# Layer 0's attention in halves: Gram blocks of 16 columns, softmax by banks, first tiles mixed ahead

## The chip, the cores and the metric

The kernel runs on one core of a Trainium2 chip. The metric is the time of one execution on the device, in microseconds (us), as the median of several runs; a profile comes from one execution of its own. TensorE (PE; its weight loads are shown as PEld) multiplies, VectorE (DVE), ScalarE (ACT) and GpSimd (POOL) do the elementwise work, and SyncE's queue (SP) issues the DMAs.

## The reference, cut to what matters

The program is two transformer layers on x of shape 4 x 512 x 1024, in fp32. Layer 0's attention, the part that the change touches, works for each of the 1024 columns on its own: the four batch rows of a column attend to each other over the 512 positions. Ahead of it the rows of x are normalised, and its result is added to x.

```python
q = jnp.transpose(x, (2, 0, 1))                       # column, n, position
scores = jnp.einsum('lnc,lmc->lnm', q, q) / c ** 0.5  # 4 x 4 for each column
prob = jax.nn.softmax(scores, axis=-1)
msg = jnp.einsum('lnm,lmc->lnc', prob, q)
return x + jnp.transpose(msg, (1, 2, 0))
```

Layer 0's FFN follows: a layer norm, a product with W_base, gate and LoRA inputs (1160 columns in all), a top-2 routing and the LoRA outputs. Then layer 1's attention with 32 heads and layer 1's FFN, which the change does not touch.

## The kernel before, in words

x lies in SBUF as 16 tiles of 128 rows by 1024 columns; tile n * 4 + j holds rows j * 128 to j * 128 + 127 of batch row n. The tiles are loaded in the order of the row blocks j (L62), so the four tiles of block 0 come first.

For each row block j the kernel takes the tiles' mean and variance (`statistics`: ACT with two passes over a tile, L111 and L113, for one or two of the four tiles, DVE with L119 and L120 for the others; then `rsqrt`, L93 to L100), and normalises the four tiles (L130) into a layout of 32 groups. A group g has 128 columns: 32 columns of x for each of the four batch rows. The first 20 groups go to `hA`, the last 12 to `hB`, of which all four row blocks are kept.

TensorE turns each group (L255), four to a PSUM tile, and ACT copies them out (L257) to `hTA` and `hTB`. It multiplies each group with itself (L259 for the 20 groups of hA, summed over the row blocks in the five PSUM banks `gA`). The 12 groups of hB are multiplied after the last row block (L267, three banks `gB`), since there is no PSUM for them before that. A Gram block is 128 x 128, of which only the entries with the same column matter: a 4 x 4 block for each column.

`weights` works on one bank of four groups: a mask times the Gram block (L195), a sum that leaves 4 x 4 scores for each column (L198), the softmax in small operations, and the weights spread out again over a 128 x 128 block with its identity added (L212, by DVE or POOL). `turned` transposes them (L219) and ACT copies them (L221). `mix` multiplies a row block of four groups by the weights (L230), and DVE adds the product to x (L233). There are 8 x 4 mixes: first all four row blocks of the 20 groups of hTA, then row block after row block of the rest.

The weights of layer 0's FFN, `w0`, come in eight chunks of 128 x 1160. Each is loaded to a stage (L168), ACT makes the rounded part (L171) and POOL the remainder (L172). The first four are loaded to memory that hA and hB leave, through two stage buffers, the last four to memory that hTA leaves, through three.

Once the first row block is mixed, the tiles of row block 0 get their statistics for the FFN (L300), and the first two tiles are normalised (L463 to L465), transposed (L152) and split (L134, L135). Then the FFN's products begin: `base` (L305) takes, for each of the three column groups of a tile, all eight chunks in order, with three products each (`matmul3`, L139 to L141). POOL adds the bias to x (L497).

A scheduler orders each engine's instructions by the program's order and its own estimates; `tc.high_priority` and `tc.issue_after` are hints to it. Engines run their queues in order.

Of the kernel before, what the change touches and what calls it, by code (L numbers as in the profile page):

```python
# [17 lines left out]
P = 128  # L18
# [15 lines left out]
GW = 32  # L34
# [11 lines left out]
def block_kernel(ctx: ExitStack, tc: tile.TileContext, a: dict, out: bass.AP):  # L46
# [31 lines left out]

    same_col = const.tile([P, GW], F32, name="same_col")
    V.tensor_copy(same_col, ident[:, 0:GW])  # L80
    for n in range(1, NB):
        V.tensor_tensor(same_col, same_col, ident[:, n * GW : (n + 1) * GW], ALU.add)
    same_n = const.tile([P, NB], F32, name="same_n")
    V.tensor_reduce(same_n, ident.rearrange("p (n l) -> p n l", n=NB), AX.X, ALU.add)
# [5 lines left out]
    def rsqrt(v, n, eps, name="y2", bufs=3):  # L90

        root = small.tile([P, n], F32, name="root")
        A.activation(root, v, AF.Sqrt, bias=epsilons[eps])  # L93
        y = small.tile([P, n], F32, name="y")
        V.reciprocal(y, root)
        t = small.tile([P, n], F32, name="nt")
        V.scalar_tensor_tensor(out=t, in0=y, scalar=-0.5, in1=y, op0=ALU.mult, op1=ALU.mult)
        V.scalar_tensor_tensor(out=t, in0=v, scalar=eps, in1=t, op0=ALU.add, op1=ALU.mult)
        y2 = small.tile([P, n], F32, name=name, bufs=bufs)
        V.scalar_tensor_tensor(out=y2, in0=t, scalar=1.5, in1=y, op0=ALU.add, op1=ALU.mult)  # L100
        return y2
# [27 lines left out]
    def normalise(dst, xt, mv, rstd, k):  # L129
        return V.tensor_scalar(dst, xt, mv[:, k, 0:1], rstd[:, k : k + 1], ALU.subtract, ALU.mult)  # L130
# [34 lines left out]
    def load_split(pool, stage, src, shape, name, eng=None):  # L165

        raw = stage.tile(shape, F32, name="stage")
        nc.sync.dma_start(out=raw, in_=src)  # L168
        hi = pool.tile(shape, FR, name=f"{name}_h")
        lo = pool.tile(shape, FR, name=f"{name}_l")  # L170
        A.copy(hi, raw)  # L171
        (eng or V).tensor_tensor(lo, raw, f32(hi), ALU.subtract)  # L172
        return hi, lo

# [3 lines left out]
    NQA, NQ = GA // 4, NGR // 4  # L178
    wpools, aside = ExitStack(), ExitStack()
    with tc.tile_pool(name="a_hTB", bufs=1) as hTBp, tc.tile_pool(name="a_WB", bufs=GB // 4) as WBp, \  # L180
# [11 lines left out]
        def weights(gram, eng):  # L192

            masked = wk.tile([P, 4 * NB, GW], F32, name="masked")
            V.tensor_tensor(masked, gram.rearrange("p g (n l) -> p (g n) l", n=NB),  # L195
                            same_col.unsqueeze(1).to_broadcast([P, 4 * NB, GW]), ALU.mult)
            sc = wk.tile([P, 4, NB], F32, name="sc")
            V.tensor_reduce(sc.rearrange("p g n -> p (g n)"), masked, AX.X, ALU.add)  # L198
            top = small.tile([P, 4, 1], F32, name="top")
            V.tensor_reduce(top, sc, AX.X, ALU.max)  # L200
            ex = wk.tile([P, 4, NB], F32, name="ex")
            V.tensor_tensor(ex, sc, top.to_broadcast([P, 4, NB]), ALU.subtract)
            exps.append(A.activation(ex, ex, AF.Exp, scale=1.0 / math.sqrt(S)))
            den = small.tile([P, 4, 1], F32, name="den")
            V.tensor_reduce(den, ex, AX.X, ALU.add)
            rden = small.tile([P, 4, 1], F32, name="rden")
            V.reciprocal(rden, den)
            pr = wk.tile([P, 4, NB], F32, name="pr")
            V.tensor_tensor(pr, ex, rden.to_broadcast([P, 4, NB]), ALU.mult)
            V.tensor_tensor(pr, pr, same_n.unsqueeze(1).to_broadcast([P, 4, NB]), ALU.add)  # L210
            wt = wk.tile([P, 4 * NB, GW], F32, name="wt", bufs=3)
            eng.tensor_tensor(  # L212
                wt, pr.rearrange("p g n -> p (g n)").unsqueeze(2).to_broadcast([P, 4 * NB, GW]),
                same_col.unsqueeze(1).to_broadcast([P, 4 * NB, GW]), ALU.mult)
            return wt.rearrange("p (g n) l -> p g (n l)", g=4)

        def turned(wt, ps, Wp):
            for g in range(4):
                T.transpose(ps[:, g, :], wt[:, g, :], ident)  # L219
            w = Wp.tile([P, 4, P], F32, name="w")  # L220
            A.copy(w, ps)  # L221
            return w

        xv = x.rearrange("p (n j) (g l) -> p j g n l", n=NB, l=GW)

        def mix(q, w, j, psp):
# [5 lines left out]
            xs = xv[:, j, 4 * q : 4 * q + 4]  # L232
            V.tensor_tensor(xs, xs, ps.rearrange("p g (n l) -> p g n l", n=NB), ALU.add)  # L233

        psA, psB = ExitStack(), ExitStack()
        with tc.tile_pool(name="a_hB", bufs=1) as hBp, tc.tile_pool(name="a_hA", bufs=2) as hAp:
            gAp = psA.enter_context(tc.tile_pool(name="a_gA", bufs=1, space=PSUM))
            hB = [hBp.tile([P, GB, P], F32, name=f"hB{j}") for j in range(TPB)]
            junk = hBp.tile([P, D], F32, name="junk")
            gA = [gAp.tile([P, 4, P], F32, name=f"gA{q}") for q in range(NQA)]  # L240
            with tc.tile_pool(name="a_pt", bufs=NQ - NQA, space=PSUM, side="right") as ptp:
                for j in range(TPB):
                    hA = hAp.tile([P, GA, P], F32, name="hA")
                    xs = [x[:, n * TPB + j, :] for n in range(NB)]
                    mv, rstd = statistics(xs, junk=[junk] * (1 + j % 2))
                    for n in range(NB):
                        for dst, c0, c1 in ((hA, 0, GA * GW), (hB[j], GA * GW, D)):
                            normalise(dst.rearrange("p g (n l) -> p n g l", n=NB)[:, n],
                                      xs[n][:, c0:c1].rearrange("p (g l) -> p g l", l=GW),
                                      mv, rstd, n)  # L250
                    for q in range(NQ):
                        pt = ptp.tile([P, 4, P], F32, name="pt")
                        for g in range(4 * q, 4 * q + 4):
                            src = hA[:, g, :] if g < GA else hB[j][:, g - GA, :]
                            T.transpose(pt[:, g % 4, :], src, ident)  # L255
                        dst = hTA[:, 4 * q : 4 * q + 4] if q < NQA else hTB[:, 4 * q - GA : 4 * q - GA + 4]
                        A.copy(dst[:, :, j * P : (j + 1) * P], pt)  # L257
                    for g in range(GA):
                        T.matmul(gA[g // 4][:, g % 4, :], lhsT=hA[:, g, :], rhs=hA[:, g, :],  # L259
                                 start=(j == 0 and g % 4 == 0), stop=(j == TPB - 1),  # L260
                                 skip_group_check=True)
            gBp = psB.enter_context(tc.tile_pool(name="a_gB", bufs=1, space=PSUM, side="right"))
            gB = [gBp.tile([P, 4, P], F32, name=f"gB{q}") for q in range(NQ - NQA)]
            for q in range(NQ - NQA):
                for g in range(4):
                    for j in range(TPB):
                        T.matmul(gB[q][:, g, :], lhsT=hB[j][:, 4 * q + g, :],  # L267
                                 rhs=hB[j][:, 4 * q + g, :], start=(j == 0 and g == 0),
                                 stop=(j == TPB - 1), skip_group_check=True)
            ws = [turned(weights(g, (G, V)[q % 2]), g, WAp) for q, g in enumerate(gA)]  # L270
# [4 lines left out]
        def load_w0(pool, chunks, bufs):  # L275
            with tc.tile_pool(name="b_st", bufs=bufs, side="right") as stage:
                for ch in chunks:
                    w0.append(load_split(pool, stage, a["w0"][ch], [P, W0_COLS[-1][1]], f"w0{ch}",
                                         G))

        load_w0(w0p, range(ND // 2), 2)
        psA.close()
        with tc.tile_pool(name="a_ps", bufs=4, space=PSUM) as psp:
            ws += [turned(weights(g, (V, G)[q % 2]), g, WBp) for q, g in enumerate(gB)]
            with tc.issue_after(exps[-1].ins):
                A.activation(first, first, AF.Sqrt)
            for q in range(NQA):
                for j in range(TPB):
                    mix(q, ws[q], j, psp)
            aside.close()  # L290
            w0q = wpools.enter_context(tc.tile_pool(name="b_wB", bufs=1, side="right"))
            jp = psB.enter_context(tc.tile_pool(name="a_junk", bufs=1))
            junk = jp.tile([P, D], F32, name="junk")
            stats0 = {}
            for j in range(TPB):
                for q in range(NQA, NQ):
                    mix(q, ws[q], j, psp)
                if j == 0:
                    with tc.high_priority():
                        stats0[0] = statistics([x[:, n * TPB, :] for n in range(NB)], junk=[junk])  # L300
                    load_w0(w0q, range(ND // 2, ND), 3)
# [3 lines left out]
    def base(hts, w, cols, pop, part):  # L305

        hh, hl = hts
        po = []
        for c0, c1 in cols[part]:
            ps = pop.tile([P, 512], F32, name="po")  # L310
            for ch in range(ND):
                wh, wl = w[ch]
                matmul3(ps[:, 0 : c1 - c0], hh[:, ch, :], hl[:, ch, :], wh[:, c0:c1],
                        wl[:, c0:c1], start=(ch == 0), stop=(ch == ND - 1))
            po.append(ps)
        return po
# [98 lines left out]
    with tc.tile_pool(name="b_h", bufs=2) as hp, tc.tile_pool(name="b_hTh", bufs=2) as hTh, \  # L415
# [45 lines left out]
        def turn0(s):  # L461
            t = order[s]
            h = hp.tile([P, D], F32, name="h")  # L463
            with tc.high_priority() if s < 2 else ExitStack():
                normed.append(normalise(h, x[:, t, :], *stats0[s // NB], s % NB))  # L465
            return transposed(h, (hTh, hTl), ptp)

        normed = []
        hts = {0: turn0(0), 1: turn0(1)}
        po = {0: base(hts[0], w0, W0_COLS, pop, slice(0, 3))}  # L470
        room1 = raw()
        fetch_w1(room1, 0)
        done, mvs0, mvs1 = normed[1], {}, {}
        for s, t in enumerate(order):
# [22 lines left out]
            G.tensor_tensor(x[:, t, :], x[:, t, :], bias0, ALU.add)  # L497
# [1100 lines left out]
```

## Time and profile before

| what | value |
|---|---|
| median of 3 runs (lowest, highest) | 1797.71 us (1795.58, 1800.64) |
| the profiled execution's own time | 1795.89 us |
| its span, first to last instruction | 1794.1 us |
| mean granted TensorE clock | 0.992 |
| TensorE busy | 1734.4 us (97%) |
| VectorE busy | 1325.2 us (74%) |
| ScalarE busy | 904.1 us (50%) |
| GpSimd busy | 884.6 us (49%) |
| first matmul | 15.53 us |
| end of the Gram products, by the chain | 62.95 us |
| first product of layer 0's FFN (L139) | 110.06 us |

All times within a profile are counted from the span's start. A line of the timeline gives the start, the duration of a group of like instructions, the engine, the line of the program, the operation, what it writes and reads, and in brackets the idle time ahead of it with what ended it. A line of the windows gives a stretch, its length and the busy time of each engine in it, with the number of instructions. An fp32 product counts as two matmul records, since TensorE takes it in two passes; a transpose counts as one.

### The profile page before, as it was taken

To read this page: it belongs to the slowest core of one execution; us is meant where nothing else is said; L and a number is where in the kernel's file an instruction comes from. 1 tells how busy PE (TensorE), PEld (TensorE's weight loads), DVE (VectorE), ACT (ScalarE), POOL (GpSimd) and SP (SyncE) were. 2 spreads that over 40 slices of the span, in tenths; PEclk is the share of its full clock that TensorE was granted. 3 is DMA by queue.
4 is the path that set the end of the run, shared out by engine and by line. 5 is a ranking of instruction groups with operands and counts; after the bars stand their busy time and mean duration, and the time that the engine had idled before them with its cause. 6 is when DMAs were issued, how large, how long until landed. Compare 5 with 4: busy or idle time off the path is not lost.

```text
span 1794.1 us, 31052 instructions
## 1 busy us (share of the span) xinstructions
PE 1734.4 (97%) x10280; PEld 1449.8 (81%) x10280; DVE 1325.2 (74%) x3556; ACT 904.1 (50%) x2321; POOL 884.6 (49%) x851
## 2 busy tenths in 40 slices
PE   6979999999899999999999999999999999989999
PEld 5979999999667877767777767777766777789998
DVE  7777887576687777777777777777678777587785
ACT  6331332165665555475555565555565555453332
POOL 0352433101456566545566545666645555565453
PEclk9989999999899999999999999999999999999999
DMA  4121554236332343362242453243344323844331
GB/s 188 70 87 62 169 173 144 75 95 186 112 121 79 121 130 105 109 201 93 98 140 92 133 174 117 92 138 106 116 166 131 125 99 115 308 170 137 130 117 61
DMA packets 131937, 228.12 MB, mean 127 GB/s; under 512 B 22272, under 2 KB 58752, under 8 KB 128448
## 3 DMA queue, kind: packets, MB, share of 16 engines
q1 hardware_dynamic: 131776, 226.13, 37.6%
q8 instruction: 82, 1.34, 0.3%
q14 instruction: 79, 0.65, 0.1%
HBM read 156.60 MB, written 71.83 MB: 127 GB/s over the span
## 4 chain that ended last, share of the span: by engine, by line
PE 84%; DVE 7%; POOL 2%; DMA 2%; ACT 2%; issue 1%; SPq 0%; POOLq 0%; DVEq 0%; ACTq 0%
PE psv L851 8%; PE pst L835 7%; PE pss L139 4%; PE pss L140 4%; PE pss L141 4%; PE poa L139 3%; PE pob L139 3%; PE po L139 3%; PE po L141 3%; PE po L140 3%; PE psq L139 3%; PE psq L141 3%; PE psq L140 3%; PE poa L141 3%; PE poa L140 3%; PE pob L141 3%
## 5 line engine op out<-in xcount | busy, mean ns | idle before, releaser
L814 ACT ACTIVATE p<-p,mn 128x512 f32<-128x512 f32 (+3 forms) x512 | 284.5, 559 | 206.7 <-DVE mn L811 205.4
L634 POOL TENSOR_TENSOR qf<-qf,ropeT 64x512 f32<-64x512 f32 x128 | 165.5, 1293 | 276.5 <-ACT qf L630 272.4
L811 DVE CUSTOM_DVE_ANT_0 p<-pss,causal 128x512 f32<-128x512 f32 (+3 forms) x512 | 231.2, 485 | 33.8 <-PE pss L141 26.1
L835 PE MATMUL pst<-ident,p 128*128 128x128 f32 x1280 | 185.8, 273 | 0.7 <-ACT pT L837 0.7
L635 POOL TENSOR_TENSOR qf<-qf,t 64x512 f32<-64x512 f32 x128 | 165.7, 1294 | 41.2 <-DVE t L633 33.2
L835 PEld LDWEIGHTS pst<-ident,p 128*128 128x128 f32 x1280 | 153.6, 141 | 25.4 <-ACT pT L837 2.5
L837 ACT COPY pT<-pst 128x512 f32<-128x512 f32 x256 | 142.0, 580 | 47.7 <-PE pst L835 46.9
L643 POOL TENSOR_TENSOR ql<-qf,qh 128x384 fp32r<-128x384 f32 x128 | 130.0, 1015 | 66.8 <-DVE qh L642 66.8
L139 PE MATMUL pss<-kT,ql 128*128 128x512 f32 (+2 forms) x384 | 144.6, 377 | 4.7 <-DVE mn L811 2.0
L886 POOL TENSOR_TENSOR cxl<-s,cxh 128x256 fp32r<-128x256 f32 x128 | 97.1, 767 | 90.1 <-ACT cxh L885 64.2
L139 PE MATMUL po<-w_h,hTl 128*128 128x384 f32 (+1 forms) x384 | 133.4, 348 | 0.8 <-DVE x L339 0.8
L140 PE MATMUL pss<-kT,qh 128*128 128x512 f32 (+2 forms) x384 | 130.9, 341 | 0.0
L141 PE MATMUL pss<-kT,qh 128*128 128x512 f32 (+2 forms) x384 | 130.5, 340 | 0.0
L141 PE MATMUL po<-w_h,hTh 128*128 128x384 f32 (+1 forms) x384 | 130.2, 339 | 0.0
L140 PE MATMUL po<-w_l,hTh 128*128 128x384 f32 (+1 forms) x384 | 129.8, 338 | 0.0
L837 DVE COPY pT<-pst 128x256 f32<-128x256 f32 x128 | 54.0, 422 | 95.9 <-PE pst L835 95.5
L630 ACT COPY qf<-psq 128x512 f32<-128x512 f32 x126 | 74.0, 587 | 70.7 <-PE psq L141 69.2
L632 DVE TENSOR_TENSOR t<-psq,ropeT 32x512 f32<-32x512 f32 x126 | 87.6, 696 | 24.6 <-ACT qf L630 20.6
L139 PEld LDWEIGHTS pss<-kT,ql 128*128 128x128 f32 x384 | 72.5, 189 | 40.0 <-POOL ql L643 11.6
L814 ACT ACTIVATION_READ_ACCUMULATOR p<-p,mn 128x1 f32 x512 | 97.4, 190 | 0.0
L633 DVE TENSOR_TENSOR t<-psq,ropeT 32x512 f32<-32x512 f32 x126 | 87.1, 691 | 1.8
L928 DVE TENSOR_TENSOR xs<-xs,pob 128x512 f32<-128x512 f32 x105 | 71.2, 678 | 19.5 <-PE pob L141 19.2
(569 smaller groups left out, 5004.0 us busy)
## 6 DMA issues: line engine op xcount, KB each, us to landing
xs<-x_d SPq DMA_DIRECT2D x128, 256.0 KB
x_d<-xs SPq DMA_DIRECT2D x128, 256.0 KB
slotC<-in_woT_dram SPq DMA_DIRECT2D x32, 512.0 KB
rb<-r_d SPq DMA_DIRECT2D x128, 128.0 KB
w_t<-raw SPq DMA_DIRECT2D x32, 288.0 KB
x<-in_x_dram SPq DMA_DIRECT2D x16, 512.0 KB
x_d<-x SPq DMA_DIRECT2D x32, 256.0 KB
slotA<-q_d SPq DMA_DIRECT2D x8, 1024.0 KB
```

The lines of the kernel that those rows point to most:

```text
L139: T.matmul(ps, lhsT=al, rhs=bh, start=start, stop=False, **kw)
L140: T.matmul(ps, lhsT=ah, rhs=bl, start=False, stop=False, **kw)
L141: T.matmul(ps, lhsT=ah, rhs=bh, start=False, stop=stop, **kw)
L634: G.tensor_tensor(f[mid], f[mid], ropeT[mid, 0, :], ALU.mult)
L635: G.tensor_tensor(f[mid], f[mid], t2[mid], ALU.add)
L643: G.tensor_tensor(l, f[:, P:S], f32(h), ALU.subtract)
L811: turn_of[0] = V.tensor_tensor_reduce(out=to, in0=ps[:, 0:n], in1=causal[:, S - n : S], scale=1.0, scalar=-NEG, op0=ALU.add, op1=ALU.min, ...
L814: A.activation(to, to, AF.Exp, bias=mn[:, i : i + 1], scale=-1.0, accum_out=rs[:, i : i + 1])
L835: T.transpose(ps[:, w : w + P], p[:, OF[i] + j * P : OF[i] + (j + 1) * P], ident)
L837: copy(pT[:, AT[js[0]] : AT[js[0]] + w], ps[:, 0:w])
L851: T.matmul(ps[n * KVR : (n + 1) * KVR, S - w : S], lhsT=k[:, j, :], rhs=pTs[u + n][:, AT[j] : AT[j] + w], start=(j == 0), stop=(j == TPB - 1))
L886: G.tensor_tensor(l, src, f32(h), ALU.subtract)
```

## The change

The groups are laid out anew: a group of 128 columns is now two halves of 64, each with 16 columns of x for the four batch rows. A Gram block is two products of 64 x 64, one on each half of the array's columns, which write to the two halves of the PSUM partitions. The 32 groups' blocks so take four PSUM banks, and all of them are summed while the row blocks come; the pool `hB` and the separate `gB` products are gone. In row blocks 0 to 2 each four transposes are followed by the eight half products of the same groups; in the last row block all half products come first, and the transposes after them.

In row block 0 the statistics are taken in two sets, three tiles and one; ACT normalises part of the tiles, and the tiles are normalised in two column halves. Later blocks' statistics are to be issued after the normalisation or the root ahead of them.

The softmax works on a bank of eight groups in place of four. The spreading by columns is made in two steps (`halves`, `wt`). As soon as a set of four groups has its weights, row block 0 of the set before is mixed; then come row blocks 1 to 3 of the groups in hTA, with the statistics of the four tiles of row block 0 between them, then the two first tiles' normalisation, then the rest of the mixes. `w0`'s first chunks are to be issued after the last `wt`. For the first tile `base` takes the first four chunks for all three column groups, then the last four. POOL's bias additions are to be issued after the last split on POOL.

```diff
-    same_col = const.tile([P, GW], F32, name="same_col")
...
+    same_col = const.tile([P, GL], F32, name="same_col")
+    V.tensor_reduce(same_col, ident.rearrange("p (k l) -> p l k", l=GL), AX.X, ALU.add)
+    same_half = const.tile([P, 2], F32, name="same_half")
+    V.tensor_reduce(same_half, ident.rearrange("p (b k) -> p b k", b=2), AX.X, ALU.add)
...
+            halves = wk.tile([P, GBK, 2, NB], F32, name="halves")
+            V.tensor_tensor(halves, pr.unsqueeze(2).to_broadcast([P, GBK, 2, NB]),
+                            same_half.unsqueeze(1).unsqueeze(3).to_broadcast([P, GBK, 2, NB]),
+                            ALU.mult)
...
+            grams = [gp.tile([P, GBK, 2 * GW], F32, name=f"g{k}") for k in range(NGR // GBK)]
+            with tc.tile_pool(name="a_pt", bufs=4, space=PSUM, side="right") as ptp:
                 for j in range(TPB):
-                    hA = hAp.tile([P, GA, P], F32, name="hA")
+                    h = hp.tile([P, NGR, P], F32, name="h")
                     xs = [x[:, n * TPB + j, :] for n in range(NB)]
-                    mv, rstd = statistics(xs, junk=[junk] * (1 + j % 2))
...
+                    sets = (xs[:3], xs[3:]) if j == 0 else (xs,)
+                    norms = []
+                    with tc.issue_after((normed if j == 1 else rooted[0]).ins) if j else ExitStack():
+                        for k, part in enumerate(sets):
+                            mv, rstd = statistics(part, "", 3, [junk] * (k == 0) * (1 + (j > 1)))
...
+                            if j == 0 and n < (2 if c else 3):
+                                normed = A.activation(to, xt, AF.Identity, bias=off[:, i : i + 1],
+                                                      scale=rstd[:, i : i + 1])
+                            else:
+                                normalise(to, xt, mv, rstd, i)
...
+                    def gram(q):
+                        for g in range(4 * q, 4 * q + 4):
+                            for b in range(2):
+                                half = slice(b * 2 * GW, (b + 1) * 2 * GW)
+                                T.matmul(grams[g // GBK][half, g % GBK, :], lhsT=h[:, g, half],
+                                         rhs=h[:, g, half], start=(j == 0 and g % GBK == 0),
+                                         stop=(j == TPB - 1), skip_group_check=True)
...
+                    for q in range(NQ):
+                        if j < TPB - 1:
+                            turn(q)
+                        gram(q)
+                    if j == TPB - 1:
+                        for q in range(NQ):
+                            turn(q)
-                    for g in range(GA):
-                        T.matmul(gA[g // 4][:, g % 4, :], lhsT=hA[:, g, :], rhs=hA[:, g, :],
...
-            for q in range(NQ - NQA):
-                for g in range(4):
-                    for j in range(TPB):
-                        T.matmul(gB[q][:, g, :], lhsT=hB[j][:, 4 * q + g, :],
...
+            for k, gram in enumerate(grams):
+                halves = weights(gram)
+                for i in range(2):
+                    q = 2 * k + i
+                    w, last_wt = turned(halves, i, psp, WAp if q < NQA else WBp, (V, G)[i])
+                    ws.append(w)
+                    if q > 0:
+                        mix(q - 1, ws[q - 1], 0, psp)
+            mix(NQ - 1, ws[NQ - 1], 0, psp)
...
+            with tc.issue_after(last_wt.ins):
+                load_w0(w0p, range(ND // 2), 2, (G, G))
+            mv = small.tile([P, NB, 2], F32, name="mv", bufs=3)
+            for k, (q, j) in enumerate((q, j) for q in range(NQA) for j in range(1, TPB)):
+                mix(q, ws[q], j, psp)
+                if k % 2 and k // 2 < NB:
+                    statistic(mv, x[:, k // 2 * TPB, :], k // 2)
+            stats0 = {0: (mv, rsqrt(mv[:, :, 1], NB, 1e-5, "rstd", 3))}
             aside.close()
...
+            load_w0(w0q, range(ND // 2, ND), 3, (G, G))
+            early = []
+            for n in range(2):
+                early.append(hp.tile([P, D], F32, name="h"))
+                done = normalise(early[n], x[:, n * TPB, :], *stats0[0], n)
+            for j in range(1, TPB):
                 for q in range(NQA, NQ):
                     mix(q, ws[q], j, psp)
...
-                    with tc.high_priority():
-                        stats0[0] = statistics([x[:, n * TPB, :] for n in range(NB)], junk=[junk])
-                    load_w0(w0q, range(ND // 2, ND), 3)
...
+        for chunks in (range(ND),) if not in_halves else (range(ND // 2), range(ND // 2, ND)):
+            for ps, (c0, c1) in zip(po, cols[part]):
+                for ch in chunks:
...
-        po = {0: base(hts[0], w0, W0_COLS, pop, slice(0, 3))}
+        po = {0: base(hts[0], w0, W0_COLS, pop, slice(0, 3), True)}
...
+            with tc.issue_after(behind_split[0].ins):
+                G.tensor_tensor(x[:, t, :], x[:, t, :], bias0, ALU.add)
```

## The prediction, made before the changed kernel ran

> **What bounds the kernel now.** I read the page's chain first, then the stages of layer 0's attention by windows, then TensorE's timeline and the chain in them. The chain is 84% TensorE:
>
> ```profile
> PE 84%; DVE 7%; POOL 2%; DMA 2%; ACT 2%; issue 1%; SPq 0%; POOLq 0%; DVEq 0%; ACTq 0%
> ```
>
> Windows (start:end, length; busy us of PE, PEld, DVE, ACT, POOL; granted clock; DMA share; GB/s):
>
> ```profile
> 0.00:15.50 15.50, 0.00 (x0) 0.00 (x1) 9.22 (x32) 9.26 (x16) 0.97 (x14) 1.00 0.89 344
> 15.50:27.40 11.90, 9.80 (x72) 9.50 (x72) 11.40 (x36) 10.74 (x21) 0.00 (x0) 1.00 0.65 258
> 27.40:52.20 24.80, 24.75 (x218) 23.82 (x219) 14.87 (x40) 14.23 (x29) 0.00 (x0) 1.00 0.01 2
> 98.50:111.40 12.90, 4.04 (x19) 3.61 (x20) 12.64 (x18) 4.10 (x6) 11.48 (x7) 0.60 0.41 152
> 111.40:300.00 188.60, 187.80 (x1113) 186.00 (x1112) 144.44 (x418) 49.58 (x104) 69.14 (x54) 1.00 0.38 128
> ```
>
> PE has nothing for 15.5 us, is full from 27.4, is nearly empty from 98.5 to 111.4, and full again after that. So whatever starts layer 0's first product (L139) sooner moves the end by as much. PE's timeline shows what lies ahead of it:
>
> ```profile
> 15.53 3.87 PE L255 MATMUL pt<-ident,hA 128*128 128x128 f32 x20 [15.53 <-DVE hA L130]
> 31.20 4.63 PE L259 MATMUL gA<-hA 128*128 128x128 f32 x40
> 52.05 10.88 PE L267 MATMUL gB<-hB 128*128 128x128 f32 x96
> 69.56 17.14 PE L230 MATMUL ps<-w,hTA 128*128 128x128 f32 x152
> 106.80 1.94 PE L152 MATMUL pt<-ident,h 128*128 128x128 f32 x8 [8.39 <-DVE x L233]
> 110.06 0.68 PE L139 MATMUL po<-w_h,hTl 128*128 128x392 f32 x1
> ```
>
> The chain puts a row block at 3.73 us of transposes and 4.47 of Gram products (8.2 in all), and gB at 10.73 after the last block; PE ends those at 62.97, the mixes at 98.4. The hole behind the mixes is the chain through tile 0's statistics:
>
> ```profile
> 96.67 2.17 DVE nt L97
> 98.84 0.60 DVE x L233
> 99.44 1.99 DVE nt L98
> 101.43 0.60 DVE x L233
> 102.03 1.99 DVE rstd L100
> ```
>
> Each of these 128x4 operations takes 0.16 us where POOL is idle (11.44 to 12.0 us); here POOL runs four weight splits in a row (93.56 to 104.0), and each takes 2.
>
> **The change, part by part.** The profiled execution took 1795.89 us, span 1794.1; the median of the runs is 1.8 above it.
>
> **Gram halves.** Before: 128 products, two passes each, at 0.112 us (4.47/40): 28.6 us. After: 256 products of 64 columns by 64 rows, 512 passes, in pairs on the two column halves. The one row of this kind is layer 1's:
>
> ```profile
> 903.34 2.37 PE L851 MATMUL psv<-pT,slotA 128*64 128x512 f32 x16
> ```
>
> That is 2,560 rows for each half (512+384+256+128, two passes). At gA's 0.87 ns a row, one half after the other would take 4.5 us; it took 2.37, so the halves run side by side. In the records partners start 7 ns apart, and one pair follows another after 429, 322, 216 and 109 ns for 512, 384, 256 and 128 rows: 107 ns for each 128 rows and about 2 more. For 64 rows that gives 55 ns; the row above it, 109, is the upper end. I take 60, near the line through four rows: 256 pair passes, 15.4 us, 13.2 saved (14.5 saved at 55, 0.7 at 109).
>
> A rule speaks against this: by the Trainium skill, TensorEngine Tiling (Array Packing), section Performance Considerations, each matmul carries some 60 cycles of overhead, and tiling should not be taken where a dimension is already small. By it (60 cycles at the 2.4 GHz that the page TensorE: Matmul & The Clock Gate gives in its first table, twice a pair) a pair pass would be about 105 ns, an estimate, and the saving nearly nothing; the 2 ns left over in the pair rows of psv speak for the lower figure.
>
> **Changes of array shape.** After a transpose, psv's first pair comes after 202 ns where the next transpose comes after 109, and its second pair is 51 late (480 for 429); on the way out 203 for 109, then 165 for 109. Sum 0.3 us a round trip. The new order is four transposes, then eight half products, eight times in three blocks, and once in the last: 25 x 0.3 = 7.5 us added.
>
> **PE by block.** 32 transposes x 0.109 = 3.5, Gram 32 x 2 x 0.06 = 3.8, shapes 8 x 0.3 = 2.4: 9.7 us, more than the 8.2 of before; but the 10.73 of gB are gone. ACT has eight copies at 0.53 and one or two tiles' statistics at 2.45 (L111, L113), so 6.7 to 9.2 us a block; DVE two or three tiles' statistics at 1.3, some 1.2 of small ones and four normalisations at 1.0 (L130's two forms), 7.8 to 9.1. Both are close under PE: a thin cover.
>
> **Start.** The constants' reductions (0.28) keep their slot in DVE's queue. Three tiles' statistics no longer wait for the fourth: the third tile's aggregate ends at 9.1 in both; a root at 0.3 and five small operations at 0.2 between two 0.65 statistics: 11.75. ACT then normalises three half tiles at 0.58 (half of L113's 1.15), DVE the fourth: 14.0, against 15.53. PE starts cold: 20 transposes took 3.87 us here and 2.45 in the next block, and four took 0.86 instead of 0.44 until 19.1, so 3.5 us at half rate cost 1.75. Blocks 0, 1 and 2 end at 25.5, 35.2 and 44.9 (the added waits put each later block's statistics behind the normalisation ahead of them in DVE's and ACT's queues; block 1's rows are still ready by 24.5: root by 19.6 behind ACT's queue, 0.8 of small ones, 4.0 of normalisation). The last block's Gram products start at G = 44.9.
>
> **Softmax.** Four banks in place of eight: four masks and four reductions at 0.62, 14 small ones at 0.08 to 0.2; first weights ready at G+8.2. Meanwhile PE ends the Gram products (G+3.9) and does the eight transposes held back, paced by ACT's copies, until G+8. Then eight steps of turning (0.44) and mixing (0.89): 10.6 us of PE; ACT's queue holds eight copies, a 1.28 table load and two weight casts at 1.16, one waiting for its DMA (3.0 us for 63.01's), ahead of copies three and four: PE is through at G+21. The other 24 mixes cost what they did: 15 at 0.89 against DVE's 15 x 0.62 and five statistics at 0.62, to G+35; nine more to G+43.
>
> **The hole.** Tile 0's statistics now run between the mixes, and the small operations and both normalisations before the last nine mixes. POOL is idle there (first four splits G+15 to G+28, the next from G+41.7), so 0.16 each. After the last mix: transposes 0.45, copy 0.6, split 0.7, hops 0.7. First product at G+45.5 = 90.4, against 110.06: 19.7 sooner.
>
> **Weights.** The last four chunks still wait for the last mix of hTA (G+35): 5.5 us to land as before, cast 1.16, then 2.66 each on POOL: G+44.4 to G+52.4. The product taken in halves needs them only after 36 products at 0.18, at G+52.6, the last at G+54.2: hidden by 1.8 us; a later landing costs its excess. The bias DMA now goes ahead of the last chunk on SP and waits for DVE: same cover. POOL's bias additions now wait behind the split of b0; tile 0's output needs them two tiles of product (26 us) later. From there on each engine's order is that of before but for a mask's memsets, a rope DMA and one copy: no give-back is seen with PE at 187.80 of 188.60.
>
> **Sum.** PE idled 1.7 and 0.6 us in 62.8 to 98.5 that sums of busy time don't show; I allow 2.2 for the like. 1795.9 - 19.7 + 2.2 = 1778.4 against the profiled run, 1780.2 against the median: 1779.
>
> **Rivals.** (1) A pair pass costs 109: blocks of 12.8, 3.1 x 4 = 12.5 us later, 1791. For: no row is shorter. Against: the four-row line. (2) Slower: the halves take turns, since four instructions must issue within 60 ns and the trace sustains 54 ns for one (transposes and their weight loads, 109 a pair of instructions), less only in bursts. At 109 a half pass the Gram products cost 55.8 instead of 15.4: 40 later, 1819. It loses from 0.06 + 17.5/256 = 0.128 us a pair pass. Against: psv's pairs start 7 ns apart. (3) ACT is the bound while x loads (copies and statistics in one queue, 9.2 of 9.7): some 2 us a block, 1785. (4) It does not do what it says: the product starts at 90 but stops for the last chunks, landing late; 3 to 6 us, up to 1785.
>
> **How the numbers follow.** Forecast 0.68; (3) and (4) 0.14; (1) 0.09; (2) 0.09. The forecast's own spread is 1770.5 (no stalls 2.2, pairs at 55 1.3, ACT not held by the DMA 2.5, shape changes at 0.2 since part of their weight loads may overlap 2.5: 8.5 less) to 1783 (4 more of stalls). The range takes in (3), (4) and (1): 1770 to 1792. A difference under 0.3% (5.4 us) is about what a measurement of this kernel can't tell from none; (1) lies near that edge and is split. Faster 0.86, same 0.05, slower 0.09.
>
> **What would show it.** Right: Gram blocks of eight half products in about 0.55 us, blocks of 9 to 10 us, last Gram product near 49, no PE gap over 2 us before the first product near 90 to 93, 128x4 operations at 0.16. Wrong: Gram records 109 ns apart; PE waiting on ACT's copies inside blocks; the product waiting for POOL's splits; the gain gone again by 300 us.

## The result, and the profile after

| kernel | median (lowest to highest), us | ratio to before, 95% interval |
|---|---|---|
| before | 1796.64 (1793.1 to 1800.64), 4 runs | 1 |
| after | 1778.96 (1777.05 to 1782.75), 4 runs | 0.9903 [0.9888, 0.9918] |

The change makes the kernel 17.7 us faster by the medians. The two profiled executions are 1795.89 and 1777.1 us, 18.8 us apart; the span after is 1775.3. The forecast was 1779. The sum behind it did not go as it was written, though: the first product came sooner than forecast, a stop that was not forecast took a good part of that back, and waits near the end of the program, which differ from run to run, made up for some of it.

The chain after:

```profile
PE 85%; DVE 7%; DMA 3%; ACT 2%; issue 1%; POOL 1%; SPq 0%; DVEq 0%; POOLq 0%; ACTq 0%
```

The windows after (columns as for before: start:end, length; busy us of PE, PEld, DVE, ACT, POOL with the number of instructions; granted clock; DMA share; GB/s):

```profile
14.00:24.00 10.00, 10.00 (x144) 7.94 (x142) 8.19 (x22) 9.65 (x19) 0.00 (x0) 1.00 0.91 361
...
85.00:92.00 7.00, 5.90 (x44) 5.62 (x43) 5.99 (x12) 4.63 (x7) 7.00 (x4) 1.00 0.53 180
...
100.00:112.00 12.00, 6.63 (x37) 6.34 (x36) 11.12 (x15) 0.45 (x2) 10.55 (x6) 0.88 0.07 25
112.00:300.00 188.00, 187.35 (x1104) 185.77 (x1103) 140.66 (x423) 51.27 (x107) 63.59 (x51) 0.99 0.39 131
```

TensorE is full while x loads, with ACT busy 9.65 of 10 us beside it. The empty stretch of before (8.4 us of nothing behind the mixes) has become 1.1 us. A new one is in 100 to 112: TensorE is busy for 6.63 of 12 us while DVE is busy for 11.12 and POOL for 10.55. TensorE's timeline after:

```profile
13.70 1.09 PE L291 MATMUL pt<-ident,h 128*128 128x128 f32 x4 [13.70 <-ACT h L283]
...
17.53 0.66 PE L291 MATMUL pt<-ident,h 128*128 128x128 f32 x4
18.12 0.69 PE L299 MATMUL g<-h 128*64 128x64 f32 x16
18.73 0.66 PE L291 MATMUL pt<-ident,h 128*128 128x128 f32 x4
...
43.36 4.42 PE L299 MATMUL g<-h 128*64 128x64 f32 x144
47.71 3.71 PE L291 MATMUL pt<-ident,h 128*128 128x128 f32 x32
52.48 1.25 PE L239 MATMUL ps<-ident,wt 128*128 128x128 f32 x8 [1.05 <-ACT hTB L293]
...
88.29 0.42 PE L143 MATMUL po<-w_h,hTl 128*128 128x392 f32 x1
...
95.13 0.34 PE L143 MATMUL po<-w_h,hTl 128*128 128x392 f32 x1
...
111.27 0.45 PE L379 MATMUL pt<-ident,hw 128*128 128x128 f32 x1 [5.37 <-issue]
...
112.16 0.52 PE L145 MATMUL po<-w_h,hTh 128*128 128x384 f32 x1
```

A round of four transposes and eight half products takes 1.2 us (17.53 to 18.73). The last Gram product ends at 47.8, where before it was 62.95. The first product stands at 88.29, where before it was 110.06: 21.8 us sooner. Then comes the stop, 5.37 us ahead of the transposition of tile 0's routed weights. Behind it the records show the products 0.32 us apart instead of 0.175, until 116: half the clock, about 2 us more. So of 21.8 us about 14 were left at 116. By the first product of layer 1's output (poa) at 436 it was 15.0, and 15.5 at 796 and at 1346. The rest, up to 18.8, was gained in the last stage: from 1500 us on TensorE's waits sum to 11.6 us before and to 10.2 after, and two windows of 100 us have a granted clock of 0.98 before, one of them after. These are not steps of the change: a second profile of the changed kernel (e5 below) has 12.9 us of such waits.

### The profile page after: what moved, and what is told of

Its sections match the earlier page's. It is cut to its first block, busy times and chain, and to the rows that moved or that the text cites. A ratio compares the mean times of both kernels' runs of the same rounds, so it can differ in the third digit from the quotient of the medians.

```text
span 1775.3 us, 31519 instructions
## 1 busy us (share of the span) xinstructions
PE 1724.4 (97%) x10536; PEld 1437.0 (81%) x10536; DVE 1315.3 (74%) x3516; ACT 904.0 (51%) x2319; POOL 884.3 (50%) x851
## 4 chain that ended last, share of the span: by engine, by line
PE 85%; DVE 7%; DMA 3%; ACT 2%; issue 1%; POOL 1%; SPq 0%; DVEq 0%; POOLq 0%; ACTq 0%
PE psv L908 9%; PE pst L892 7%; PE pss L143 4%; PE pss L144 4%; PE pss L145 4%; PE po L143 4%; PE po L145 3%; PE po L144 3%; PE poa L143 3%; PE pob L143 3%; PE psq L143 3%; PE psq L145 3%; PE psq L144 3%; PE poa L144 3%; PE poa L145 3%; PE pob L145 3%
## 5 line engine op out<-in xcount | busy, mean ns | idle before, releaser
L894 ACT COPY pT<-pst 128x512 f32<-128x512 f32 x256 | 141.7, 580 | 47.5 <-PE pst L892 46.7
```

The source lines that it names most:

```text
L894: copy(pT[:, AT[js[0]] : AT[js[0]] + w], ps[:, 0:w])
```

## Experiments

Theory A, formed on the trace of after: the stop is DVE's routing of tile 0, held by POOL. DVE's timeline after, first the root of tile 0's statistics (read further down), then the stretch of the stop, and POOL's timeline beside the stop:

```profile
77.61 0.15 DVE L101 SCALAR_TENSOR_TENSOR nt<-y 128x4 f32<-128x4 f32 x1
77.80 0.16 DVE L102 SCALAR_TENSOR_TENSOR nt<-mv,nt 128x4 f32<-128x4 f32 x1
...
78.50 0.16 DVE L104 SCALAR_TENSOR_TENSOR rstd<-nt,y 128x4 f32<-128x4 f32 x1
...
97.52 0.17 DVE L513 COPY lg<-po 128x8 f32<-128x8 f32 x1 [2.12 <-issue]
...
98.37 2.16 DVE L491 TENSOR_SCALAR one<-eq,key 128x8 f32<-128x8 f32 x1
100.56 2.32 DVE L496 SCALAR_TENSOR_TENSOR rest<-one,lg 128x8 f32<-128x8 f32 x1
102.92 0.16 DVE L484 TENSOR_REDUCE best<-rest 128x1 f32<-128x8 f32 x1
103.11 2.11 DVE L486 SCALAR_TENSOR_TENSOR eq<-rest,best,rank 128x8 f32<-128x8 f32 x1
...
108.20 2.38 DVE L507 TENSOR_SCALAR rw<-one,w 128x8 f32<-128x8 f32 x1
...
110.88 0.29 DVE L376 TENSOR_TENSOR hw<-po,rw 128x128 f32<-128x128 f32 x1
```

```profile
83.05 10.57 POOL L176 TENSOR_TENSOR w_l<-stage,w_h 128x1160 fp32r<-128x1160 f32 x4 [10.11 <-ACT w_h L175]
...
98.08 2.42 POOL L176 TENSOR_TENSOR b_l<-stage,b_h 128x1024 fp32r<-128x1024 f32 x1 [3.24 <-ACT b_h L175]
100.46 7.05 POOL L554 TENSOR_TENSOR x<-x,bias 128x1024 f32<-128x1024 f32 x3
107.47 0.78 POOL L445 TENSOR_TENSOR raw<-raw 128x288 fp32r<-128x288 f32 x1
108.22 2.33 POOL L554 TENSOR_TENSOR x<-x,bias 128x1024 f32<-128x1024 f32 x1
```

At 98.08 stands the split of b0, the weights of the LoRA outputs; L554 are the bias additions. Each long operation on eight elements ends 0.02 to 0.03 us after an instruction of POOL does: 100.53 after 100.50, 102.88 after 102.86, 105.23 after 105.20, 107.54 after 107.51, 110.58 after 110.55. The reductions between them take 0.16 throughout. So each instruction of POOL lets one of these operations of DVE through. The routing begins at 97.5 and ends at 111.17, and TensorE goes on at 111.27: the "issue" of the profile is this wait, without its name. The rival, theory B, was that the stop is TensorE's own.

The Trainium skill has this in SBUF — State Buffer, section Who interferes with whom: DVE and GpSimd share a pair of SBUF ports as an exclusive lock, and the second to issue is blocked for the whole instruction; DVE operations with two SBUF inputs, or in a two-port mode (which tensor_scalar can enter), are concerned, and tensor_reduce never is. The rows agree, down to the reductions; that ports are the reason no run here shows.

**e1, POOL's bias additions behind the routing.**

```diff
+            if s < 2:
+                with tc.issue_after(weighed[0].ins):   # the last operation of route
+                    V.tensor_copy(bias0[:, 0:1], bias0[:, 0:1])
```

> The changed kernel, but the bias additions of POOL can't start before tile 0 is routed (and from tile 1 on not before tile 1 is): a copy of one column of the bias onto itself, put behind DVE's last routing operation, is what they wait for. Theory A: the stop of TensorE at 105.9 us (5.4 us, called issue, in front of the transposition of tile 0's routed weights) is DVE's routing, whose small operations with a per-partition scalar (0.23 us when POOL is idle) took 2.1 to 2.4 us each while POOL ran the split of b0 and the bias additions, 98.1 to 110.6. Then only the split of b0 still collides, the routing ends near 103, the stop is under 0.5 us, the granted clock does not fall after it, and the time is 1771 to 1773 against the changed kernel's 1777 to 1783. Theory B: the stop is TensorE's own issue (or another wait that the profile does not name): it stays at 5 us and the time at 1777 to 1780.

Measured: 1773.77 us (1772.79 to 1775.05), ratio 0.9875 [0.9858, 0.9891]. DVE's timeline of e1:

```profile
98.50 2.45 DVE L486 SCALAR_TENSOR_TENSOR eq<-lg,best,rank 128x8 f32<-128x8 f32 x1
...
103.47 0.23 DVE L508 SCALAR_TENSOR_TENSOR rw<-one,w,rw 128x8 f32<-128x8 f32 x1
```

Only the operation beside the split of b0 (98.51 to 100.93) is long. The routing takes 5.9 us (98.1 to 104.0) instead of 13.7, TensorE has no gap there, and the granted clock stays at 1.00 in 88 to 130, where it was 0.92. Theory A holds and B falls. The time is a little over the expected 1771 to 1773.

**e2, tile 0's product not in halves.**

```diff
-        po = {0: base(hts[0], w0, W0_COLS, pop, slice(0, 3), True)}
+        po = {0: base(hts[0], w0, W0_COLS, pop, slice(0, 3))}
```

> The changed kernel with tile 0's product not taken in halves: the chunks run 0 to 7 for each of the three column groups, as before the change. Theory A: the halves hide about 1.2 us (the last chunk is split at 93.6, and the product would need it at 92.4), but they put the end of the first column group, which the routing reads, from 4.4 us after the product's start to 8.8, so that the routing meets the bias additions. Without them the routing starts near 95.4, runs mostly ahead of POOL's split of b0 at 98.1, and ends by 101: the stop at 105.9 is gone, a wait of 1 to 2 us for the last chunk stands in front of 94, and the time is 1772 to 1775. Theory B: the halves are what keeps the product going, and the stop has another cause: the wait for chunks is 3 us or more, the stop stays, 1780 or more.

Measured: 1773.6 us (1771.47 to 1775.01), ratio 0.9875 [0.986, 0.9889], as theory A has it. Waits of TensorE in e2 (in total, times, longest), then lines of ACT's timeline:

```profile
PE po L144 <- POOL w_l L176: 0.8, 1, 0.8
PE pt L379 <- PE po L145: 0.6, 1, 0.6
```

```profile
99.25 1.05 ACT L175 CAST b_h<-stage 128x1024 fp32r<-128x1024 f32 x1 [6.93 <-DMA stage<-in_b0T_dram]
...
100.65 1.28 ACT L500 ACT_TABLE_LOAD   x1
101.94 0.20 ACT L500 ACTIVATE e<-e 128x1 f32<-128x1 f32 x1
```

What the halves hide is 0.8 us of waiting for a chunk. The routing began at 95.7, and its first eleven operations were through at 97.9, before POOL's split of b0. But it did not end by 101, as expected: its exponential stood in ACT's queue behind the cast of b0, which waited for its DMA. The last two scalings then met the bias additions, and the routing ended at 107.8. That is 3.3 us sooner than in the changed kernel, and TensorE came to it 1.4 later (the wait for the chunk, and a first product at 88.7), so 0.6 us of the stop was left.

**e3, tile 0's statistics behind the mixes.** The eight `statistic` operations, the root and the two normalisations are issued after the last mix (`tc.issue_after(mixed.ins)`).

> The changed kernel with tile 0's statistics, their root and the two normalisations behind the last mix on DVE, instead of among the mixes; the order of mixing is kept. Theory: after the last mix (86.3) DVE has eight statistics of 0.62, the root and three operations of 0.16, or up to 2 each where they meet POOL's weight splits (until 94.9), and two normalisations of 1.0 to 1.2: first product at 98 to 101 instead of 88.3. The routing is then later than most bias additions of POOL, so the stop at 105.9 goes: 10 to 12 lost, 5 to 6 regained, 1781 to 1785. Rival: the hole is closed by the mixing order alone (the mixes of the first rows come first) and the place of the statistics is worth little: first product before 93, 1777 to 1780.

Measured: 1788.25 us (1785.2 to 1789.83), ratio 0.9955 [0.994, 0.997]; first product at 101.5, against 88.3. The rival falls; the first product is 0.5 us and the time 3 us over the theory's ranges. The stop is gone (the routing of 112.3 to 115.7 has no long operation), but two waits of TensorE, of 9.5 and 2.5 us, stand ahead of the first product, and the clock in 88 to 130 is 0.84. DVE's timeline of e3:

```profile
93.33 1.04 DVE L101 SCALAR_TENSOR_TENSOR nt<-y 128x4 f32<-128x4 f32 x1
94.41 0.72 DVE L102 SCALAR_TENSOR_TENSOR nt<-mv,nt 128x4 f32<-128x4 f32 x1
95.16 0.16 DVE L104 SCALAR_TENSOR_TENSOR rstd<-nt,y 128x4 f32<-128x4 f32 x1
```

The first ends at 94.37; POOL's last split of a chunk ends at 94.35.

**e4, no pairs of half products.** Of each four groups the products of one half come first, then those of the other.

```diff
-                        for g in range(4 * q, 4 * q + 4):
-                            for b in range(2):
+                        for b in range(2):
+                            for g in range(4 * q, 4 * q + 4):
```

> The changed kernel with the same half products in another order: of each four groups first the four on the lower column half, then the four on the upper, so that neighbours share a half and can't run side by side but where the halves change. Theory: the halves run side by side in the changed kernel (about 57 ns a pair pass); here a round of eight half products takes 0.9 to 1.1 us instead of 0.61, with 32 rounds 9 to 16 us more before the softmax; last Gram product near 58 to 62 instead of 47.8, first product at 97 to 104, of which the stop at 105.9 gives some 5 back: 1781 to 1790. Rival: a pass of 64 rows is short by itself and nothing is shared: rounds stay at 0.61 and the time at 1777 to 1780.

Measured: 1789.87 us (1785.94 to 1790.38), ratio 0.9961 [0.9947, 0.9976]; first product at 96.7. TensorE's timeline of e4:

```profile
19.42 0.97 PE L299 MATMUL g<-h 128*64 128x64 f32 x16
20.32 0.66 PE L291 MATMUL pt<-ident,h 128*128 128x128 f32 x4
```

Eight half products keep TensorE for 0.90 us (19.42 to 20.32) instead of 0.61 (18.12 to 18.73), and the last Gram product is 8.3 us later, less than the 9 to 16 expected. The single records say why. Neighbours on the same half follow each other after 58 ns. Where the half changes, three passes of the new half start within 3 to 6 ns of passes of the old one. In a round there is one such change, so 16 passes take 13 times 58 ns instead of 8 times; in the last block, with one every eight passes, they take ten. That is 24 x 0.29 and 8 x 0.12, 7.9 of the 8.3 us. The halves do run side by side. The stop stayed (5.5 us), against what was expected of it: the split of b0 and the bias additions had moved along with the mixes.

**e5 to e8, on one chip.** e5 is the changed kernel again; e6 has the edits of e1 and e2; e7 has all transposes of a row block ahead of its half products; e8 has the edits of e7 and e1.

```diff
-                    for q in range(NQ):
-                        if j < TPB - 1:
-                            turn(q)
-                        gram(q)
+                    if j < TPB - 1:
+                        for q in range(NQ):
+                            turn(q)
+                    for q in range(NQ):
+                        gram(q)
```

> The changed kernel once more, as the measure for its neighbours on the same chip. Expected: the stop of 5.4 us before the transposition of tile 0's routed weights is there again, first product near 88.5, time 1777 to 1780.

> The changed kernel with both remedies at once: POOL's bias additions wait for the routing, and tile 0's product is not taken in halves. Theory: both remove the same stop, so they don't add up: 1772 to 1775, as each alone (1773.8 and 1773.6), the routing of tile 0 ends before 104, and about 1 us of waiting for the last weight chunk stands in the product. Rival: they are two costs that add: 1768 to 1770.

> The changed kernel with all 32 transpositions of a row block ahead of all its half products, instead of four and eight by turns, in the first three blocks. Theory: 21 changes of array shape go, each worth 0.3 us (a round is 1.205 us, of which four transpositions take 0.44 and eight half products 0.47). TensorE's blocks could go from 9.6 us to 7.5; but ACT then has 6.7 to 9.2 us a block and its statistics stand among the copies, so some waits on ACT's copies appear and 2 to 4 of the 6.3 us come through: last Gram product at 44 to 46, first product at 84.5 to 86.5; the stop of 5.4 us stays or moves with it: 1774 to 1777. Rival: ACT's copies and statistics set the pace in the changed kernel too (the ACT rival of the prediction): the last Gram product stays at 47 to 48.5 and the time at 1777 to 1780.

> The grouped row blocks and the bias additions behind the routing together. Theory: the two have nothing to do with each other and add up: whatever the grouping alone gains over the changed kernel, and 5 us from the stop: 1769 to 1772. Rival: the layer's weights and bias land no sooner, so a part of what the grouping gains is lost again to waits for the weight chunks or the split of b0: 1773 or more.

| run | median (lowest to highest), us | ratio to before | last Gram product starts | first product | stop |
|---|---|---|---|---|---|
| e5 | 1781.9 (1778.61 to 1783.38) | 0.9919 [0.9907, 0.9932] | 47.8 | 88.6 | 5.7 |
| e6 | 1775.06 (1773.71 to 1777.07) | 0.9884 [0.9871, 0.9898] | 49.0 | 89.7 | none |
| e7 | 1782.31 (1781.02 to 1785.32) | 0.9926 [0.9912, 0.9939] | 47.5 | 88.3 | 5.7 |
| e8 | 1774.32 (1771.9 to 1775.48) | 0.9878 [0.9864, 0.9891] | 47.3 | 88.0 | none |

e5 came out above its 1777 to 1780. e6 against e5: the two remedies don't add up; either takes the stop away. e6's routing ended at 105.1, a little after the expected 104, and 0.7 us of waiting for a chunk stands in its product. On this chip that is worth 6.8 us (e6) and, from e7 to e8, 8.0 us: the stop of 5.7 and about 2 of half clock. e7 against e5: grouping brings nothing, so its theory falls and its rival holds, with DVE named beside ACT (the time, like e5's, lies over the rival's 1777 to 1780). TensorE's timeline of e7:

```profile
26.72 1.94 PE L291 MATMUL pt<-ident,h 128*128 128x128 f32 x16 [3.23 <-DVE mv L118]
...
43.81 3.95 PE L299 MATMUL g<-h 128*64 128x64 f32 x128 [1.45 <-DVE h L134]
```

What TensorE saves in changes of shape (21 x 0.3 = 6.3 us by the working further down) it mostly waits, 3.2 and 1.5 us, for the next block's statistics and normalisation. e8 gains what the bias additions alone give, not the sum that was expected; its rival's 1773 or more was met, but not for the rival's reason, since the grouping had gained nothing that could be lost again.

**e9, the softmax's steps in the order of before.** All sets of weights are turned first; then the mixes of hTA over all rows, then those of hTB, with tile 0's statistics as soon as its rows are mixed.

> The changed kernel with the softmax's steps in the order of before: all eight sets of weights are turned first, then the mixes of hTA bank by bank over all rows, then those of hTB, with tile 0's statistics, their root and the two normalisations as soon as the first rows are mixed. The Gram halves, all Gram products while x loads, the softmax by banks and the product in halves stay. Theory: the first rows are complete only after 23 of 32 mixes, near 81, and the statistics (8 at 0.62), the remaining mixes (9 at 0.62), the small operations (up to 2 each beside POOL's weight splits of 83 to 94) and the normalisations (2.2) then share DVE: first product at 94 to 99 instead of 88.3, and the small operations of the root take 1 to 2.4 us each again. The routing comes later than part of POOL's bias additions, so the stop of 5.4 shrinks to 0 to 4: 1780 to 1787. Rival: the mixing order is worth little beside the early Gram products: first product at 91 or before, 1777 to 1781.

Measured: 1786.61 us (1781.43 to 1789.67), ratio 0.9937 [0.9914, 0.996]; first product at 101.4, later than the 94 to 99 expected. TensorE waits 4.8 us behind the mixes and 2.2 among them for DVE. No stop is left ahead of the transposition of the routed weights. DVE's timeline of e9, beside POOL's four splits of 86.25 to 96.69:

```profile
89.82 1.71 DVE L101 SCALAR_TENSOR_TENSOR nt<-y 128x4 f32<-128x4 f32 x1
...
92.05 2.08 DVE L102 SCALAR_TENSOR_TENSOR nt<-mv,nt 128x4 f32<-128x4 f32 x1
...
94.65 2.06 DVE L104 SCALAR_TENSOR_TENSOR rstd<-nt,y 128x4 f32<-128x4 f32 x1
```

As they stand, these times split the 21.8 us at the first product: 8.7 (110.06 to 101.4) come from the Gram products and what goes with them, 13.1 (101.4 to 88.3) from the order of the mixes with the statistics among them. But e9's last Gram product starts at 49.5, 1.9 us later than in the changed kernel, though e9's edit lies behind it. Counted from that product, the order is worth about 11 us.

## Why the prediction was right, and where it was not

**Pair pass, right.** Forecast 60 ns, between 55 and 109. In the records of the last block partners start 7 ns apart and the next pair 58.4 ns after the first. The rule of the Trainium skill that was weighed (TensorEngine Tiling (Array Packing), Performance Considerations: some 60 cycles a matmul, about 105 ns a pair by the estimate) is not what these rows show, and rivals 1 and 2 fall. e4 shows that the pairs share the time.

**Changes of shape and blocks, right.** Forecast 0.3 us a round trip and 9.7 us a block. A round is 1.202 us, less 4 x 0.109 and 8 x 0.0584 leaves 0.30; eight rounds are 9.62.

**Start, right to 1.0 us.** First matmul at 13.70 for 14.0. The last block's products start at 43.9 for 44.9: the slow clock ended with the second round and cost 1.4 us for 1.75, and three blocks took 0.1 less each.

**The thin cover, right.** ACT was put at 6.7 to 9.2 us a block and was busy 9.65 of 10 in 14 to 24. The ACT rival (3) did not come about, but e7 shows how near it is: without the shape changes, statistics and normalisations set the pace.

**Softmax and mixes, right to 1.2 us.** Counted from G = 43.9: first turning G+8.6 (forecast G+8), turning and mixing over at G+20.4 (G+21), fifteen mixes at G+33.8 (G+35), nine more at G+42.0 (G+43), first product G+44.4 (G+45.5).

**The hole, right.** The operations on 128x4, about 2 us each before, run ahead of POOL's second set of splits and take 0.15 to 0.16 (77.61 to 78.66 in DVE's timeline after). e3 prices the place of the statistics at 13 us at the first product, e9 that place together with the order of the mixes at 13; counted from the last Gram product, which was later in both, they are 12 and 11.

**The weights, right.** The product in halves never waited for a chunk; the last split ended at 93.6, 1.5 us ahead of the second half (95.13). Rival 4 fell: a stop of the size that it named did come, but not for the chunks.

**"No give-back is seen", wrong: this is the step that failed.** It asked who waits for the bias additions' result (tile 0's output, much later) and for the chunks, and found both covered. It did not ask what the additions hold up while they run, nor what the halves put off. The routing reads tile 0's first column group, and its result is due when tile 1's first column group is done. Before, the routing began 5.4 us after the first product (115.45) and was due 17.8 after it (127.9). With halves it began 9.2 after it (97.5) and was due 17.6 after it (105.9): a window of 8.4 us in place of 12.4, and in it POOL's split of b0 and the bias additions. The two causes meet there; with either gone, the stop is gone or nearly so, as e1 and e2 show. The lines were in the profile of before; DVE's timeline, and POOL's, there:

```profile
115.84 2.31 DVE L431 SCALAR_TENSOR_TENSOR eq<-lg,best,rank 128x8 f32<-128x8 f32 x1
...
118.38 2.13 DVE L436 TENSOR_SCALAR one<-eq,key 128x8 f32<-128x8 f32 x1
...
122.52 0.29 DVE L321 TENSOR_TENSOR hw<-po,rw 128x128 f32<-128x128 f32 x1
```

```profile
105.42 5.19 POOL L497 TENSOR_TENSOR x<-x,bias 128x1024 f32<-128x1024 f32 x2 [1.42 <-DVE h L130]
...
115.73 4.75 POOL L497 TENSOR_TENSOR x<-x,bias 128x1024 f32<-128x1024 f32 x2
```

There the first two bias additions ran in the hole (105.42 to 110.6) and only two operations of the routing were held; its result came at 122.8, 5 us ahead of its time. The change also issues the additions after the last split on POOL, which keeps them out of the time before the split of b0. No run takes this hint away, so what it costs by itself stays open. The prediction had read the 2 us operations in the hole as POOL's doing and had not carried that to the next place where they stand beside POOL.

**The sum.** The allowance for stalls was 2.2 us; the stop and the slow clock behind it took about 7.5. The first product was 2.1 us better than forecast, and the late waits made up the rest. That 1779 was met is partly luck: the errors had opposite signs, and the late waits belong to no step of the forecast. The whole 21.8 us off the profiled time of before would give 1774, and e1, e2, e6 and e8, with the stop gone or nearly so, lie at 1773.6 to 1775.1.

**A version that beats both** is the changed kernel with either remedy. The one of e2 is the simpler, a change of one argument: 1773.6 us, ratio 0.9875 [0.986, 0.9889] to before. Neither remedy alone ran on the chip of e5; on that one the two together (e6, at most 1777.07) stand clear of the changed kernel (e5, at least 1778.61).

## What to carry to other kernels

When a step moves to another place, ask of each of its instructions not only who waits for its result, but what it holds up while it runs: here POOL's additions let one small operation of DVE through for each 2.3 us. When an order is changed to hide a wait, look up who reads the first part of the result: the halves hid 0.8 us and took 4 from the routing's window. And a stop that the profile calls issue may still have a plain cause in another engine's timeline, in the row that ends 0.1 us before it.

## What the runs showed of the hardware

- A pass of 64 rows on one half of the columns follows another on the same half after 58 ns (e4), and after as much when a partner runs on the other half (58.4 ns, the changed kernel). Where the half changes in e4, passes of the new half start within 3 to 6 ns of passes of the old one, three at each change.
- Going from transposes to half products and back cost 0.30 us, in each of the rounds of 1.202 us; hardly any of it is seen in the time once statistics and normalisation are the bound (e7).
- Small operations of DVE with two inputs in SBUF, or scaled by a per-partition value, ended 0.02 to 0.03 us after the POOL instruction beside which they were issued (five in the changed kernel, three in e9); the reductions among them took 0.16 us all the same.
- After a gap of 5.4 us TensorE ran at half rate for 4.7 us (products 0.32 us apart instead of 0.175).
